# Second layer: the causal mask in spare rows of the exponent products, three products a round, and the second right side copied whole

## The chip, the cores and the metric

The kernel runs on one core of a Trainium2 chip, in one launch. The metric is the device time of that launch in microseconds (us). Engines are named as in the profile: PE (TensorE; PEld is its weight load), DVE (VectorE), ACT (ScalarE), POOL (GpSimd) and SP (SyncE), whose queue issues most of the transfers; POOL issues some too. Each engine works through its own instructions in order and waits on semaphores of the others.

## The reference

Two layers, each an attention over a context and a feed-forward part, on x of 8 x 256 tokens of width 512. Only the second layer's attention (an mLSTM with 16 heads of 32) is touched. For each batch row b and head:

```
ig = x_cat @ Wi + bi;   fg = x_cat @ Wf + bf
F  = cumsum(log_sigmoid(fg))
log_D[s,t] = F[s] - F[t] + ig[t]   for t <= s, else -inf
D  = exp(log_D - max_t log_D)
C  = (q @ k.T / sqrt(32)) * D
h  = (C / max(|sum_t C|, exp(-max))) @ v, then normed over each head
```

Row s attends to keys t <= s only. With 256 tokens cut in two halves of 128, the pair (second half of the keys, first half of the queries) is all masked and never computed; (first keys, first queries) and (second keys, second queries) hold the diagonal and need the mask; (first keys, second queries) needs none.

## The kernel before

The launch runs through these stages in the profile: the first layer's attention (to about 225 us), the first layer's feed-forward part with ternary weights, token tile by token tile, t = 0 to 15 (`layers_joined`, to about 357 us), the second layer's attention in 32 rounds (`layer1_rounds`, 357 to 503 us), and the second layer's shared and routed experts (to the end). In the second and third the order on every engine is written out by hand: `between(n, place)` looks up in the table `places` what else is issued at a given place of round n, and the profile's order is the program's.

A round n stands for one (b, k): batch row b = n // 4 and a group k = n % 4 of four heads. Its steps are spread over rounds: `decays` (round n) builds the exponents log_D - max with a product on PE and takes exp on ACT into a tile xe; `weights` (round n + 1) makes the products of queries and keys (pqk) and multiplies them by xe on DVE into ct; `heads` and `copied` (n + 2) make num and copy it; `back` (n + 3) turns it back. The per-row work that follows when a batch row is complete is `tail`: the head norms with a reciprocal root worked out on POOL (`rsqrt_aside`, L117 to L122), `scaled` and `attended` on POOL (L840, L847, L848: they add the result to x), layer-norm statistics on DVE (L129, L130, L923, L924), then the next b's root starts.

The exponent of a pair (t, s) is a sum of six numbers per head: three bf16 parts of the key's F and ig, three of the query's. `decays` gets it from one product: the stationary side `left` (g.left[b % 2], 128 rows x k x 256 keys) holds the key's parts in rows 0 to 11 (three parts for each of four heads) and ones in rows 12 to 14; the moving side `right` (g.right[b % 2], rows x k x head x 256 queries) holds in rows 0 to 11 a 0/1 pattern that picks the head, and in rows 12 to 14 the query's parts. KR = 15 rows are used, and rows 15 to 127 are zero on `left`. The mask is a second product on top, in the same PSUM tile pd: the identity times `lateb` (128 x 128, -1e30 where a query comes before a key), repeated over the heads. `decays` makes three such pairs of products and three exps of 128 x 512 a round: heads 0 and 1, first keys, all 256 queries, mask over the first 128 of each head (256 columns); the same for heads 2 and 3; and all four heads, second keys, second queries, mask over all 512 columns.

`lefts(b)` and `rights(b)` load the parts on SP's queue from `parts_d` in DRAM, where the gate chain has put them; for b = 0 they are issued in tile t = 15 of the feed-forward part, just ahead of the transposing transfer of the hidden tile of t = 14 (`hidden_rounded`, L1159, hq), for b + 1 in round 4b + 2. PE's product `output(14)` (py, L1165, 11 matmuls) stands in round 0 between the first two and the third exponent product, and waits for that transfer; `output(15)` stands at (2, 0).

There are two `left` tiles and two `right` tiles. The second `right` is made by `second_right` at place (2, 2), in the storage of the ternary weights w2 (tag wq2, free after `output(15)`): POOL sets 128 x 2048 words to zero, copies rows 0 to 11 from the first right by a transfer, and loads and scales `lns`. The storage of w3 (`held[1]`, free after the products of t = 15) serves as the third xe buffer `at["third"]`, taken by every n with n % 3 == 2; the others take the two buffers of the tag xe, which the feed-forward tiles' h used before.

`layer1_constants` makes lateb, the head pattern, and the left tiles on POOL at the start of the second stage; `layer1_right(k)` copies the head pattern into the four k of the first `right` on ACT, one each at t = 2 to 5.

Of the kernel before, what the change touches and what calls it, by code (L numbers as in the profile page):

```python
# [19 lines left out]
F32 = mybir.dt.float32  # L20
BF16 = mybir.dt.bfloat16
# [4 lines left out]
ALU = mybir.AluOpType  # L26
# [4 lines left out]
P = 128  # L31
D = 512
KD = D // P
B = 8
S = 256
T = B * S
NT = T // P
CH = 512
# [4 lines left out]
NF = FF // P  # L43
H1 = 16
HD1 = 32
# [606 lines left out]
HG = 4  # L652
KR = 3 * HG + 3


def layer1_constants(g, wp):
    nc = g.nc
    g.lateb = wp.tile([P, P], BF16, tag="lateb", name="lateb")
    nc.gpsimd.memset(g.lateb, 0.0)
    nc.gpsimd.affine_select(  # L660
        out=g.lateb, in_=g.lateb, compare_op=ALU.is_ge, fill=-1e30, base=0, pattern=[[1, P]], channel_multiplier=-1
    )
    g.head = wp.tile([P, HG], F32, tag="head", name="head")
    nc.gpsimd.memset(g.head, 0.0)
    for part in range(3):
        nc.gpsimd.affine_select(
            out=g.head, in_=g.head, compare_op=ALU.not_equal, fill=1.0, base=-HG * part, pattern=[[-1, HG]],
            channel_multiplier=1,
        )

    g.left = [wp.tile([P, KD, S], BF16, tag=f"left{n}", name=f"left{n}") for n in range(2)]
    g.right = [wp.tile([P, KD, HG, S], BF16, tag="right0", name="right0")]
    for left in g.left:
        nc.gpsimd.memset(left, 0.0)
        nc.gpsimd.memset(left[:KR], 1.0)
# [12 lines left out]
def layer1_rounds(g, tc, gates, work, ps, qp):  # L688
# [7 lines left out]
    def opened(held):  # L696
        row = 2 * H1 * (HD1 + 1)
        first = g.ctxT[0].rearrange("p k t -> p (k t)")
        for t in (held[0][:, :row], held[0][:, row : 2 * row], first[:, :row]):
            hid_of.append(t.rearrange("p (j h d) -> p j h d", j=2, h=H1))  # L700
        gates.em = held[0][:, 2 * row : 2 * row + 2 * P].rearrange("p (n q) -> p n q", n=2)
        at["third"] = held[1][:, : HG * (S + P)].rearrange("p (r s) -> p r s", r=HG)
        at["squared"] = held[1][:, HG * (S + P) :][:, : 2 * H1 * HD1]

    def second_right():
        more = qp.tile([P, NF * D // 2], F32, tag="wq2", name="held2")
        half = KD * HG * S // 2
# [4 lines left out]
        g.lns = more[:, half : half + D]  # L712
# [25 lines left out]
    def decays(b, k):  # L738


        keys, rows = g.left[b % 2][:, k], g.right[b % 2][:, k]
        if (b * KD + k) % 3 < 2:
            xe = work.tile([P, HG, S + P], F32, tag="xe", name="xe")
        else:
            xe = at["third"]

        def part(lhsT, rhs, late, out):
            pd = ps.tile([P, CH], F32, tag="dec", name="pd", bufs=2)
            n = rhs.shape[-1]
            pd = pd.rearrange("p (r s) -> p r s", s=n)  # L750
            nc.tensor.matmul(pd, lhsT=lhsT, rhs=rhs, start=True, stop=False)
            nc.tensor.matmul(
                pd[:, :, :P], lhsT=g.identb, rhs=lateb.unsqueeze(1).to_broadcast([P, CH // n, P]),
                start=False, stop=True,
            )
# [312 lines left out]
    class Rounds:  # L1068
        def second_right(self):
            second_right()  # L1070

        def lefts(self, b):
            lefts(b)

# [22 lines left out]
def layers_joined(g, tc, qp, gates):  # L1097
# [5 lines left out]
    with tc.tile_pool(name="f0a1", bufs=2, reuse_waits="tile") as work, tc.tile_pool(name="f0a1ps", bufs=1, space=PSUM, reuse_waits="tile") as ps:  # L1103
# [153 lines left out]
        with tc.manual_schedule(engines={E_.PE, E_.Activation, E_.DVE, E_.Pool, E_.SP}):  # L1257
# [15 lines left out]
            for t in range(NT):  # L1273
                front = t - 3
                roots = {6: 3, 7: 3, 10: 7}.get(t)
                if t:
                    hidden_scale(t - 1)
                products(t, 0)
                if 0 <= front < NT - 5:
                    added(front)  # L1280
                if t + 2 < NT:
                    largest(("x", t + 2), xn[t + 2])
                silu(t, 0)
                turn_next()
                gate_steps(t, 0)
                if t in (11, 12):
                    copy_next()
                if t:
                    shifted(("h", t - 1), h[t - 1])
                gated(t, 0)  # L1290
                if front >= NT - 5:
                    added(front)
                copy_next()
                if t == 11:
                    norm_next()
                if t + 2 < NT:
                    input_scale(t + 2)
                if front >= 0:
                    stats(front)
                rooted(roots, 3 if roots == 7 else 2)  # L1300
                gate_steps(t, 1)
                if t == 15:
                    rounds.lefts(0)
                    rounds.rights(0)
                products(t, 1)
                silu(t, 1)
                if t == 12:
                    gates.queries((0, 1))
# [49 lines left out]
            def turned(tag, engine=None):  # L1358
# [529 lines left out]
```

## Time and profile before

| what | value |
|---|---|
| median of 3 runs | 1054.01 us (1052.76 to 1054.7) |
| the profiled execution | 1053.98 us, span 1051.8 us, mean granted PE clock 0.984 |
| busy in the span: PE, DVE, ACT, POOL | 998.3, 532.3, 404.9, 394.3 us |
| the rounds, 357 to 503 us | 32 rounds; last exponent product 492.4 us |
| mask products (L752) in the rounds | 96, 29.5 us as single instructions |
| exponent products (L751) | 96, 35.0 us as single instructions |
| exps (L756) | 96, 53.8 us |
| second right: POOL memset, copy of 12 rows | 372.60 us for 1.81 us; issued 374.69 us |
| ACT's copies into the first right (L685) | 4, 1.03 us each, 246.4 to 268.9 us |

A matmul's own time in the profile holds its way through the array, so neighbours overlap; what a product adds to a row of products is read from the distance of starts in the timeline. A line such as `[1.66 <-DMA hq<-hq]` in the timeline is idle time of the engine just ahead of the instruction and what ended it. In the views by window, the columns are the window, its length, the busy time (and number of instructions) of PE, PEld, DVE, ACT and POOL, the clock granted to PE as a share of full speed, the busy share of the 16 DMA engines, and GB/s.

### The profile page before, as it was taken

To read this page: it belongs to the slowest core of one execution; us is meant where nothing else is said; L and a number is where in the kernel's file an instruction comes from. 1 tells how busy PE (TensorE), PEld (TensorE's weight loads), DVE (VectorE), ACT (ScalarE), POOL (GpSimd) and SP (SyncE) were. 2 spreads that over 40 slices of the span, in tenths; PEclk is the share of its full clock that TensorE was granted. 3 is DMA by queue.
4 is the path that set the end of the run, shared out by engine and by line. 5 is a ranking of instruction groups with operands and counts; after the bars stand their busy time and mean duration, and the time that the engine had idled before them with its cause. 6 is when DMAs were issued, how large, how long until landed. Compare 5 with 4: busy or idle time off the path is not lost.

```text
span 1051.8 us, 14757 instructions
## 1 busy us (share of the span) xinstructions
PE 998.3 (95%) x5210; PEld 607.5 (58%) x5210; DVE 532.3 (51%) x1417; ACT 404.9 (38%) x692; POOL 394.3 (37%) x452
## 2 busy tenths in 40 slices
PE   6999999979999899998998999999999999999994
PEld 5766666534444356665443445556666667778772
DVE  6546566679997768787828942112112121212120
ACT  4453443447687757876321001221222222221211
POOL 0023443450000114888203045554555556454522
PEclk9999999999999999999899999999999999999997
DMA  9663433323421411241112447777777778899972
GB/s 344 229 208 135 142 108 136 110 56 60 72 57 39 90 38 48 69 137 39 50 60 91 160 145 194 176 194 189 190 206 208 204 210 231 215 246 236 245 192 36
DMA packets 101011, 152.41 MB, mean 145 GB/s; under 512 B 39576, under 2 KB 42264, under 8 KB 100892
## 3 DMA queue, kind: packets, MB, share of 16 engines
q1 hardware_dynamic: 81984, 106.78, 32.4%
q0 software_dynamic: 18944, 44.60, 19.2%
q8 instruction: 43, 0.70, 0.3%
q14 instruction: 40, 0.33, 0.1%
HBM read 110.42 MB, written 32.96 MB: 136 GB/s over the span
## 4 chain that ended last, share of the span: by engine, by line
PE 74%; DVE 13%; POOL 4%; ACT 3%; issue 3%; DMA 1%; SPq 0%; POOLq 0%; DVEq 0%; ACTq 0%
PE po L1638 14%; PE pg L1621 13%; PE pu L1621 13%; PE pw L365 5%; PE pz L400 5%; PE pt L1678 3%; PE p L1118 2%; PE pgu L990 2%; DVE ct L779 2%; PE py L1165 2%; DVE h L1131 1%; PE pv L299 1%; DVE am L1135 1%; PE s L342 1%; PE pq L333 1%
## 5 line engine op out<-in xcount | busy, mean ns | idle before, releaser
L1626 DVE TENSOR_TENSOR act<-pu,sg 128x264 f32<-128x264 f32 (+22 forms) x68 | 31.9, 469 | 313.2 <-PE pu L1621 313.2
L1663 POOL DMA_INDIRECT xg<-h_d,tok_of x85 | 83.4, 981 | 197.9 <-DVE of L1673 64.8
L1682 POOL DMA_INDIRECT out_x<-eo,to x85 | 133.0, 1564 | 55.1 <-ACT eo L1720 34.4
L1638 PE MATMUL po<-w,act 128*128 128x512 f32 (+10 forms) x456 | 143.1, 489 | 0.0
L1621 PE MATMUL pg<-xT,w 128*128 128x216 f32 (+21 forms) x512 | 134.8, 406 | 0.8 <-issue 0.8
L1720 ACT ACTIVATE eo<-po,slotw 128x512 f32<-128x512 f32 (+10 forms) x114 | 65.6, 576 | 177.0 <-PE po L1638 170.6
L1621 PE MATMUL pu<-xT,w 128*128 128x216 f32 (+21 forms) x512 | 133.3, 403 | 0.0
L1621 PEld LDWEIGHTS pg<-xT,w 128*128 128x128 f32 x512 | 93.2, 190 | 33.2 <-issue 17.8
L1621 PEld LDWEIGHTS pu<-xT,w 128*128 128x128 f32 x512 | 96.8, 190 | 26.2 <-issue 5.6
L1625 ACT ACTIVATE sg<-pg 128x264 f32<-128x264 f32 (+22 forms) x68 | 28.5, 419 | 202.9 <-PE pg L1621 178.8
L1118 PE MATMUL p<-wq,xqT 128*128 128x512 bf16 (+1 forms) x384 | 81.2, 361 | 7.0 <-DVE qi L1139 6.2
L1638 PEld LDWEIGHTS po<-w,act 128*128 128x128 f32 (+10 forms) x456 | 54.2, 154 | 57.4 <-issue 47.9
L386 POOL TENSOR_TENSOR y<-y,gam 128x512 f32<-128x512 f32 x16 | 20.2, 1265 | 138.8 <-DVE y L83 138.8
L1118 PEld LDWEIGHTS <-xqT 128*128 128x128 bf16 x384 | 37.2, 98 | 49.4 <-issue 12.5
L1679 DVE TENSOR_TENSOR xT<-pt,nw 128x512 f32<-128x512 f32 (+12 forms) x85 | 51.1, 601 | 20.5 <-PE pt L1678 20.5
L400 PE MATMUL pz<-wo,wyT 128*128 128x512 f32 x128 | 59.5, 609 | 1.3 <-ACT wyT L395 1.3
L365 PE MATMUL pw<-wg,xnT 128*128 128x512 f32 x128 | 57.8, 594 | 0.0
L1678 PEld LDWEIGHTS pt<-ident,xg 128*128 128x128 f32 (+15 forms) x340 | 39.1, 140 | 23.9 <-PE po L1638 10.5
L129 DVE BATCH_NORM_STATS2 st<-x 128x6 f32<-128x512 f32 x64 | 43.9, 686 | 12.0 <-POOL x L848 6.3
L1678 PE MATMUL pt<-ident,xg 128*128 128x128 f32 (+15 forms) x340 | 47.2, 260 | 0.7 <-DVE xT L1679 0.6
L779 DVE SCALAR_TENSOR_TENSOR ct<-pqk,xe 128x768 f32<-128x768 f32 x44 | 40.0, 951 | 8.4 <-PE pqk L775 7.9
L1165 PE MATMUL py<-wq,hq 128*128 128x512 bf16 x176 | 42.3, 391 | 1.7 <-DMA hq<-hq 1.7
(336 smaller groups left out, 1680.7 us busy)
## 6 DMA issues: line engine op xcount, KB each, us to landing
w<-in_w SPq DMA_DIRECT2D x32, 1024.0 KB
w<-in_w SPq DMA_DIRECT2D x32, 512.0 KB
wst<-in_w1T SPq DMA_DIRECT2D x8, 704.0 KB
wst<-in_w3T SPq DMA_DIRECT2D x8, 704.0 KB
wst<-in_w2T SPq DMA_DIRECT2D x6, 768.0 KB
x<-in_x SPq DMA_DIRECT2D x16, 256.0 KB
ctxT<-in_ctxT_d SPq DMA_DIRECT2D x4, 1024.0 KB
raw<-in_ctx SPq DMA_DIRECT2D x16, 256.0 KB
```

The lines of the kernel that those rows point to most:

```text
L365: nc.tensor.matmul(pw, lhsT=xnT[c][:, k, o : o + P], rhs=wg[:, k, :], start=k == 0, stop=k == KD - 1)
L400: nc.tensor.matmul(pz[i], lhsT=wyT[i][:, k, :], rhs=wo[:, k, :], start=k == 0, stop=k == KD - 1)
L779: nc.vector.scalar_tensor_tensor(ct[:, r : r + 2, :], pqk[:, :, : S + P], 1.0 / math.sqrt(HD1), xe[:, r : r + 2, :], ALU.mult, ALU.mult,)
L1118: nc.tensor.matmul(both[:, m, : z - a], lhsT=xqT[:, k, :], rhs=w[:, k, a:z], start=k == 0, stop=k == KD - 1)
L1165: nc.tensor.matmul(py[t], lhsT=hqT[t][0][:, f, :], rhs=w2[:, f, :], start=f == 0, stop=f == NF - 1)
L1621: nc.tensor.matmul(pp[:, :n], lhsT=w[:, k, cols], rhs=xT[:, k, :n], start=k == 0, stop=k == KD - 1)
L1638: nc.tensor.matmul(po[h * at : h * at + n, :cols], lhsT=act[:, m, j * P : j * P + n], rhs=w[:, m, h * cols : (h + 1) * cols], start=m == 0 ...
L1663: nc.gpsimd.indirect_dma_start(out=xg[:n], out_offset=None, in_=h_d, in_offset=bass.IndirectOffsetOnAxis(ap=g.tok_of[:n, r, j : j + 1], ax ...
L1678: nc.tensor.transpose(pt[:, k, :n], xg[:n, k * P : (k + 1) * P], g.ident[:n, :n])
L1679: nc.vector.tensor_mul(xT, pt[:, :, :n], g.nw.unsqueeze(2).to_broadcast([P, KD, n]))
L1682: return nc.gpsimd.indirect_dma_start(out=g.out, out_offset=bass.IndirectOffsetOnAxis(ap=rows, axis=0), in_=eo, in_offset=None, compute_op ...
L1720: nc.scalar.activation(eo[:n, at : at + cols], po, AF.Copy, scale=w[r][:n, j : j + 1])
```

## The change

The mask of the diagonal pairs moves into rows 15 to 127 of the exponent product itself: `left` gets -1e30 in row p where the key's number in its half is p, and `right` gets 1 in row p for the queries s < p. That covers the keys 15 to 127; the first 15 rows are in use, so keys 0 to 14 still need a mask product, of KR - 1 = 14 query columns a head (lateb is cut to 128 x 14; 56 columns a product). The pair (first keys, second queries) must not have these rows: a third kind of stationary tile `open` (two of them, first half of the keys only) has the parts and ones in 15 rows and zeros below. A round now makes one product a pair of halves over all four heads: left x first queries with the small mask, open x second queries without a mask, left x second queries with the small mask. The exps stay three of 128 x 512.

`open` needs three more small transfers per batch row on SP's queue (12 rows of 256 bytes each, in `lefts`). The constants take more work on POOL (masked rows of both left tiles, and a whole head pattern with mask rows in k = 0 of the first right); ACT copies that k into the other three at t = 3 to 5, and nothing at t = 2. The second right is no longer set to zero: `second_right` moves to (0, 2), into the storage of w3, and copies rows 0 to 11 and rows 15 to 127 (113 rows of 8 KB) by two transfers of POOL's queue. The third xe buffer moves into the storage of w2, is set up at (2, 2), and is taken by n % 3 == 0 except n = 0.

```diff
+def opened_rows(g, n):
+    g.nc.gpsimd.memset(g.open[n], 0.0)
+    g.nc.gpsimd.memset(g.open[n][:KR], 1.0)
 def layer1_constants(g, wp):
-    g.lateb = wp.tile([P, P], BF16, tag="lateb", name="lateb")
+    g.lateb = wp.tile([P, KR - 1], BF16, tag="lateb", name="lateb")
...
+    g.open = [wp.tile([P, KD, P], BF16, tag="open0", name="open0")]
+    opened_rows(g, 0)
+    for left in g.left:
+        nc.gpsimd.memset(left, 0.0)
+        nc.gpsimd.affine_select(
+            out=left.rearrange("p k (j t) -> p (k j) t", t=P), in_=left.rearrange("p k (j t) -> p (k j) t", t=P),
+            compare_op=ALU.not_equal, fill=-1e30, base=0, pattern=[[0, 2 * KD], [-1, P]], channel_multiplier=1,
+        )
+        nc.gpsimd.memset(left[:KR], 1.0)
+    g.right = [wp.tile([P, KD, HG, S], BF16, tag="right0", name="right0")]
+    rows = g.right[0][:, 0]
+    nc.gpsimd.memset(rows, 0.0)
+    under = rows.rearrange("p r (j s) -> p (r j) s", s=P)
+    nc.gpsimd.affine_select(
+        out=under, in_=under, compare_op=ALU.is_ge, fill=1.0, base=0, pattern=[[0, 2 * HG], [1, P]], channel_multiplier=-1
+    )
+    nc.gpsimd.memset(rows[:KR], 0.0)
     for part in range(3):
         nc.gpsimd.affine_select(
-            out=g.head, in_=g.head, compare_op=ALU.not_equal, fill=1.0, base=-HG * part, pattern=[[-1, HG]],
+            out=rows, in_=rows, compare_op=ALU.not_equal, fill=1.0, base=-HG * part, pattern=[[-1, HG], [0, S]],
             channel_multiplier=1,
         )
 def layer1_right(g, k):
-    g.nc.scalar.copy(g.right[0][:, k], g.head.unsqueeze(2).to_broadcast([P, HG, S]))
+    g.nc.scalar.copy(g.right[0][:, k], g.right[0][:, 0])
 def opened(held):
-        at["third"] = held[1][:, : HG * (S + P)].rearrange("p (r s) -> p r s", r=HG)
-        at["squared"] = held[1][:, HG * (S + P) :][:, : 2 * H1 * HD1]
+        at["held"] = held[1]
+    def third():
+        more = qp.tile([P, NF * D // 2], F32, tag="wq2", name="held2")
+        at["third"] = more[:, : HG * (S + P)].rearrange("p (r s) -> p r s", r=HG)
+        at["squared"] = more[:, HG * (S + P) :][:, : 2 * H1 * HD1]
     def second_right():
-        more = qp.tile([P, NF * D // 2], F32, tag="wq2", name="held2")
         half = KD * HG * S // 2
-        nc.gpsimd.memset(more[:, :half], 0.0)
-        right = more[:, :half].bitcast(BF16).rearrange("p (k r s) -> p k r s", k=KD, r=HG)
-        nc.gpsimd.dma_start(out=right[: 3 * HG], in_=g.right[0][: 3 * HG])
+        right = at["held"][:, :half].bitcast(BF16).rearrange("p (k r s) -> p k r s", k=KD, r=HG)
+        for rows in (slice(0, 3 * HG), slice(KR, P)):
+            nc.gpsimd.dma_start(out=right[rows], in_=g.right[0][rows])
...
+        opened_rows(g, 1)
 def lefts(b):
...
+        for part in range(3):
+            nc.sync.dma_start(
+                out=g.open[b % 2][HG * part : HG * (part + 1)],
+                in_=parts_d[0, part, b * H1 : (b + 1) * H1, :P].rearrange("(k r) s -> r k s", r=HG),
+            )
 def decays(b, k):
-        if (b * KD + k) % 3 < 2:
+        n = b * KD + k
+        if n % 3 or n == 0:
             xe = work.tile([P, HG, S + P], F32, tag="xe", name="xe")
...
-        for r in range(0, HG, 2):
-            part(keys[:, :P], rows[:, r : r + 2, :], lateb, xe[:, r : r + 2, :S])
+        part(keys[:, :P], rows[:, :, :P], xe[:, :, :P])
+        part(g.open[b % 2][:, k], rows[:, :, P:], xe[:, :, P:S], False)
         yield xe
-        part(keys[:, P:], rows[:, :, P:], lateb, xe[:, :, S:])
+        part(keys[:, P:], rows[:, :, P:], xe[:, :, S:])
 layers_joined
-                if 2 <= t < 2 + KD:
+                if 2 < t < 2 + KD:
                     layer1_right(g, t - 2)
-                (0, 2): [partial(times, 1, first)],
+                (0, 2): [partial(times, 1, first), rounds.second_right],
-                (2, 2): [rounds.second_right],
+                (2, 2): [rounds.third],
```

More of the change, by code (lines that the diff above doesn't have):

```diff
@@ L653 @@
 KR = 3 * HG + 3
+def opened_rows(g, n):
+    g.nc.gpsimd.memset(g.open[n], 0.0)
+    g.nc.gpsimd.memset(g.open[n][:KR], 1.0)
 def layer1_constants(g, wp):
     nc = g.nc
-    g.lateb = wp.tile([P, P], BF16, tag="lateb", name="lateb")
+    g.lateb = wp.tile([P, KR - 1], BF16, tag="lateb", name="lateb")
     nc.gpsimd.memset(g.lateb, 0.0)
     nc.gpsimd.affine_select(
-        out=g.lateb, in_=g.lateb, compare_op=ALU.is_ge, fill=-1e30, base=0, pattern=[[1, P]], channel_multiplier=-1
+        out=g.lateb, in_=g.lateb, compare_op=ALU.is_ge, fill=-1e30, base=0, pattern=[[1, KR - 1]], channel_multiplier=-1
     )
-    g.head = wp.tile([P, HG], F32, tag="head", name="head")
-    nc.gpsimd.memset(g.head, 0.0)
+    g.left = [wp.tile([P, KD, S], BF16, tag=f"left{n}", name=f"left{n}") for n in range(2)]
+    g.open = [wp.tile([P, KD, P], BF16, tag="open0", name="open0")]
[15 more added lines that the diff above has]
+    nc.gpsimd.memset(rows[:KR], 0.0)
     for part in range(3):
         nc.gpsimd.affine_select(
-            out=g.head, in_=g.head, compare_op=ALU.not_equal, fill=1.0, base=-HG * part, pattern=[[-1, HG]],
+            out=rows, in_=rows, compare_op=ALU.not_equal, fill=1.0, base=-HG * part, pattern=[[-1, HG], [0, S]],
             channel_multiplier=1,
         )
[L671 to L675, printed above, removed]
     g.turn = wp.tile([P, HG, HD1 + 1], F32, tag="turn", name="turn")
@@ L701, in opened @@
         gates.em = held[0][:, 2 * row : 2 * row + 2 * P].rearrange("p (n q) -> p n q", n=2)
-        at["third"] = held[1][:, : HG * (S + P)].rearrange("p (r s) -> p r s", r=HG)
-        at["squared"] = held[1][:, HG * (S + P) :][:, : 2 * H1 * HD1]
+        at["held"] = held[1]
[3 more added lines that the diff above has]
+        at["squared"] = more[:, HG * (S + P) :][:, : 2 * H1 * HD1]
     def second_right():
-        more = qp.tile([P, NF * D // 2], F32, tag="wq2", name="held2")
         half = KD * HG * S // 2
-        nc.gpsimd.memset(more[:, :half], 0.0)
-        right = more[:, :half].bitcast(BF16).rearrange("p (k r s) -> p k r s", k=KD, r=HG)
-        nc.gpsimd.dma_start(out=right[: 3 * HG], in_=g.right[0][: 3 * HG])
+        right = at["held"][:, :half].bitcast(BF16).rearrange("p (k r s) -> p k r s", k=KD, r=HG)
+        for rows in (slice(0, 3 * HG), slice(KR, P)):
+            nc.gpsimd.dma_start(out=right[rows], in_=g.right[0][rows])
         g.right.append(right)
-        g.lns = more[:, half : half + D]
+        g.lns = at["held"][:, half : half + D]
+        g.open.append(at["held"][:, half + D :][:, : KD * P // 2].bitcast(BF16).rearrange("p (k t) -> p k t", k=KD))
+        opened_rows(g, 1)
         nc.gpsimd.dma_start(out=g.lns, in_=g.ln_scale.partition_broadcast(P))
@@ L745, in decays, with part @@
             xe = at["third"]
[L747 to L755, printed above, removed]
+        def part(lhsT, rhs, out, masked=True):
+            pd = ps.tile([P, CH], F32, tag="dec", name="pd", bufs=2).rearrange("p (r s) -> p r s", s=P)
+            nc.tensor.matmul(pd, lhsT=lhsT, rhs=rhs, start=True, stop=not masked)
+            if masked:
+                few = lateb.shape[-1]
+                nc.tensor.matmul(
+                    pd[:, :, :few], lhsT=g.identb, rhs=lateb.unsqueeze(1).to_broadcast([P, HG, few]),
+                    start=False, stop=True,
+                )
             nc.scalar.activation(out, pd, AF.Exp)
-        for r in range(0, HG, 2):
-            part(keys[:, :P], rows[:, r : r + 2, :], lateb, xe[:, r : r + 2, :S])
+        part(keys[:, :P], rows[:, :, :P], xe[:, :, :P])
+        part(g.open[b % 2][:, k], rows[:, :, P:], xe[:, :, P:S], False)
         yield xe
-        part(keys[:, P:], rows[:, :, P:], lateb, xe[:, :, S:])
+        part(keys[:, P:], rows[:, :, P:], xe[:, :, S:])
         yield xe
@@ L1070, in second_right, with third @@
             second_right()
+        def third(self):
+            third()
         def lefts(self, b):
```

## The prediction

> **What bounds the kernel now.** I read the page's head first: PE is busy 998.3 of 1051.8 us, which says little of a stage. Then the busy time by window over the rounds, the only stage whose instructions change much:
>
> ```profile
> 400.00:410.00 10.00, 9.92 (x119) 6.40 (x117) 9.54 (x18) 5.84 (x14) 1.68 (x4) 1.00 0.03 8
> 480.00:500.00 20.00, 16.88 (x206) 11.47 (x206) 14.90 (x25) 13.05 (x28) 17.88 (x29) 1.00 0.11 41
> ```
>
> At 400 us DVE (third busy figure) is as full as PE; at 480 POOL (fifth) is the fullest. A full PE does not decide here, so next the chain of waits in that stretch (start, length, what):
>
> ```profile
> 481.05 0.70 DVE st L129
> 481.87 1.19 DVE var L833
> 483.06 1.73 DVE ct L779 x2
> 484.79 0.61 DVE st L129
> ...
> 487.05 0.30 POOL var L117
> ...
> 496.06 1.20 POOL x L848
> 497.29 0.70 DVE st L129
> ```
>
> From one `st` to the next, 16.2 us for four rounds, there is only DVE and POOL: statistics, the root, `scaled`, `attended`, statistics again. The `st` that closes a lap starts at 434.27, 449.73, 465.17, 481.05 and 497.29 in the timeline: laps of 15.4 to 16.2 us. So PE's time is hidden from 434 on. POOL's part of that lap begins with L117 at 424.67, after DVE work that runs without a gap from here:
>
> ```profile
> 398.07 1.82 DVE L779 SCALAR_TENSOR_TENSOR ct<-pqk,held 128x768 f32<-128x768 f32 x2 [1.65 <-PE pqk L775]
> ```
>
> This is the last place where DVE waits over 1 us for PE before that unbroken run. What PE saves before 398.07 moves the rest forward; what it saves later does not.
>
> **What PE saves.** One undisturbed round in PE's timeline:
>
> ```profile
> 429.16 0.39 PE L751 MATMUL pd<-held,left 128*128 128x512 bf16 x1
> 429.39 0.27 PE L752 MATMUL pd<-lateb,identb 128*128 128x256 bf16 x1
> 429.50 0.38 PE L751 MATMUL pd<-held,left 128*128 128x512 bf16 x1
> 429.71 0.27 PE L752 MATMUL pd<-lateb,identb 128*128 128x256 bf16 x1
> 429.82 0.63 PE L807 MATMUL back<-turn,numT 128*128 128x132 f32 x4
> 430.35 0.38 PE L751 MATMUL pd<-held,left 128*128 128x512 bf16 x1
> 430.56 0.38 PE L752 MATMUL pd<-lateb,identb 128*128 128x512 bf16 x1
> 430.87 0.73 PE L771 MATMUL pqk<-qT,ctxT 32*128 32x256 f32 x8
> ```
>
> By distance of starts the masks take 0.11, 0.11 and 0.31 us, the products 0.22 each. The three products stay. Two masks of 56 columns replace three; no such row exists. From above one costs what the 256-column one does, 0.11; from below 56/256 of it, 0.02. I take 0.10, since each stands between two weight loads of 98 ns (L752 PEld, mean) that so short a product cannot cover. About 0.10 of the third mask's 0.31 is the way into the next load and stays. Saved a round: 0.53 - (0.10 + 0.20) = 0.23, from 0.20 to 0.39; I use 0.25.
>
> Where it counts: round 0's third product and round 1 (0.35 together: ACT's exp waited 1.15 us for that mask), round 2 up to pqk at 373.33 (0.25), then nothing, because DVE's root of the last tiles (376 to 379.6) releases qT and PE's num waits 0.89 for it at 380.47; then rounds 4, 5 and 6 (0.75). Sum 1.35, with the per-round bounds and the ACT-bound places 0.8 to 2.1. I take **-1.3**. The other 25 rounds save 6.3 us of PE that the DVE and POOL laps hide; without that cover they would be worth all of it.
>
> **What the moved copy costs.** `second_right` goes to (0, 2). Its first transfer waits for PE's last reader of w3, which ends as py(13) starts, 354.71. POOL is free since 351.8, so it issues at 354.9 and, at 0.61 us an issue (L710), the 113 rows at 355.5. In the packet records of the trace data follows the issue by 1.2 us (vc_d) to 2.0 us (the 12 rows of before): from 356.7 to 357.5. There stands:
>
> ```profile
> 356.28 1.41 SPq L1159 DMA_TRANSPOSE hq<-hq  x1
> 358.20:359.80 1.60, 0.00 (x0) 0.00 (x0) 1.53 (x5) 0.35 (x1) 0.00 (x0) 1.00 0.89 175
> 359.86 4.23 PE L1165 MATMUL py<-wq,hq 128*128 128x512 bf16 x11 [1.66 <-DMA hq<-hq]
> 360.40:363.80 3.40, 3.40 (x10) 1.22 (x8) 3.13 (x13) 2.98 (x4) 0.00 (x0) 0.50 0.18 67
> q0 software_dynamic: 112, 0.36, 10.7%
> ```
>
> The transposing transfer of tile 14 keeps the DMA engines 0.89 busy, PE has nothing to do but wait for it, and then runs py(14) at half clock: 11 matmuls in 4.2 us that take 2.5 elsewhere. Whatever delays hq delays everything. The last line (POOL's queue, 374 to 384 us) prices the copy: 0.36 MB took 10.7% of 16 engines for 10 us, 17 engine-us; 113 rows of 8 KB are 0.93 MB, 44 engine-us, or 2.8 us of all 16. If it queues behind hq it costs 0; if hq gets nothing until it is through, 2.8. I take half of that and a little, 1.6, as both are under way together. Then PE's clock: with py starting at 361.5, a clock back at 363.8 ends it at 365.1 (+1.2); a second half-speed stretch ends it at 366.2 (+2.3), with up to 0.6 more in what follows. In 500.3 to 503.7 PE was busy 2.46 of 3.40 us and the next 3.4 us were still at 0.50, and here it would be busy 2.3 of 3.4. So I take **+2.0**, with 0 and +4.2 as ends.
>
> [...]
>
> **The rest.** POOL's constants grow: about 8 memsets and selects of 1024 columns more (memset 0.95 us each, L674; a select of 128 columns 0.30, so 0.3 to 2.4 for 1024, I take 1.1). They ended at 235.05, now near 243.5, at worst 252; ACT first reads them at 254.5, so the cover is 10 us. But POOL then runs beside DVE, and one and the same DVE operation (L823) lasts 181 ns at best and 1469 beside POOL. Two or three such stalls of 1 us could fall on tiles 1 and 2, where PE has products ahead: 0 to 1.5, I take **+0.3**. ACT's copy dropped at t = 2 (1.03 us) frees ACT where it then waits 1.82 for PE: 0. The three `open` transfers add 0.9 us on SP (0.30 each, as `left`) between 354.74 and hq's issue; `right` already waited until 355.21 for parts_d, and hq for ACT until 356.26, so they fit with 0.3 to spare (0 to +0.3); raw behind them is needed at 374.8. In later batch rows nothing follows them for two rounds. The new wait of POOL holds back only its memsets, lns (first used at 416) and the `open` loads of b = 1 on SP at 365. xe of round 2 now waits for ct of round 0, which ends at 370.65 where the exp starts at 370.56: 0.1, hidden.
>
> Sum on the profiled 1053.98: -1.3 + 2.0 + 0.3 = +1.0, so 1055.0; the median, 1054.01, is the same.
>
> **The rivals.**
> - *The copy starves hq (34%).* Every small packet of hq waits behind an 8 KB one for the full 2.8 us: py starts at 362.7, at half clock throughout, 4.7 us, ends at 367.4 instead of 363.9: +3.5, and with the port stalls and -1.3 about +2.6 to +4: 1057.2. For it: hq's packets are many and small. It decides from about 2.3 us of delay to hq. Slower.
> - *The copy misses hq (18%).* Its data start after 359.2, or transfers share without loss: -1.3 + 0.3, to 1051.9 at best: 1052.9. For it: the 12 rows of before started 2.0 us after issue and lns 2.9.
> - *PE is the bound in all rounds (12%).* The page's 74% PE in the chain would say so: 32 x 0.25 = 8, less 1 to 2 for hq: 1047. Against it: the laps, and `st` waiting for POOL 6.3 us in five places.
> - *My forecast (36%)*: a partial delay, 1053.4 to 1056.2.
>
> **How the numbers follow.** About 0.2% (2.1 us) is what can be told from no change. The forecast gives 28 within it, 8 slower; the starved case 33 slower, 1 within; the missed one 12 within, 6 faster; the PE bound 12 faster. So faster 0.18, same 0.41, slower 0.41. The range leaves out the PE bound and the worst of the starved case: 1051.9 to 1058.0.
>
> **What would show it.** The start of py(14), 359.86 before: 361 to 362 for the forecast, 362.5 or later for the starved case, unchanged for the missed one. The granted clock from 360 to 367. The place of DVE's ct of 398.07: 1 us later on balance, and the same distances of `st` from there on. PE's idle time in later rounds should grow by 0.25 a round. I am wrong if laps shorten below 15.4 us, or if DVE operations around 240 us lengthen by more than 1.5 us together.

## The result, and the profile after

| | before | after |
|---|---|---|
| median of 4 runs, us | 1054.36 | 1068.22 |
| profiled execution, its span | 1051.8 | 1066.6 |
| granted TensorE clock | 0.984 | 0.977 |
| start of py(13), of py(14) | 354.71, 359.86 | 357.92, 373.96 |
| the ct with which DVE's unbroken run begins | 398.07 | 411.40 |
| first pgu | 505.40 | 518.67 |

The ratio is 1.0136, with an interval of 1.0122 to 1.0150: slower by 14 us, and outside the range. By the table 3.2 us are lost before py(13), 10.9 more between py(13) and py(14), 0.8 comes back up to ct, nothing changes until pgu, and 1.5 go behind it. The two losses have places of their own. The later one first, in the timeline of the kernel after (start, length, engine, instruction, and in brackets the idle time before it and what ended it):

```profile
357.92 2.54 PE L1196 MATMUL py<-wq,hq 128*128 128x512 bf16 x11
...
358.38 1.16 POOL L730 DMA_DIRECT2D held<-right  x2 [3.38 <-PE p L1149]
...
359.49 4.22 SPq L1190 DMA_TRANSPOSE hq<-hq  x1
...
373.96 4.61 PE L1196 MATMUL py<-wq,hq 128*128 128x512 bf16 x11 [10.37 <-DMA hq<-hq]
```

SP issues the transposing transfer 1.57 us after py(13) starts, exactly as before (356.28 against 354.71). What follows is not as before: the issue sits 4.22 us in the queue where it took 1.41, and PE waits 10.37 us for the data where it waited 1.66. The busy time by window (PE, PEld, DVE, ACT, POOL, granted clock, DMA share, GB/s) shows what the chip does meanwhile, and the two lower rows answer to those of 400 and 480 us:

```profile
361.00:373.60 12.60, 0.62 (x3) 0.23 (x3) 6.30 (x22) 3.93 (x4) 0.19 (x1) 0.64 1.12 144
374.00:378.40 4.40, 4.40 (x12) 1.54 (x12) 0.00 (x0) 0.00 (x0) 1.29 (x1) 0.53 0.78 186
413.33:423.33 10.00, 9.72 (x117) 6.55 (x115) 9.54 (x18) 5.59 (x14) 1.69 (x4) 1.00 0.03 9
493.27:513.27 20.00, 16.01 (x199) 10.87 (x191) 14.89 (x25) 12.52 (x27) 17.89 (x29) 1.00 0.11 41
```

For 12.6 us PE does 0.62 us of work while the DMA engines count as more than full (a share of 1.12) and move only 144 GB/s; then py(14) runs at half clock. In the lower rows DVE and POOL are as full as before, and PE has more idle time: 16.01 busy of 20 us, where it had 16.88. So the products did get cheaper, and it bought nothing there. DVE's own rows say the same:

```profile
411.40 1.82 DVE L807 SCALAR_TENSOR_TENSOR ct<-pqk,xe 128x768 f32<-128x768 f32 x2 [1.46 <-PE pqk L803]
...
463.02 0.69 DVE L129 BATCH_NORM_STATS2 st<-x 128x6 f32<-128x512 f32 x1 [1.42 <-POOL x L876]
...
478.47 0.69 DVE L129 BATCH_NORM_STATS2 st<-x 128x6 f32<-128x512 f32 x1 [1.69 <-POOL x L876]
...
494.34 0.69 DVE L129 BATCH_NORM_STATS2 st<-x 128x6 f32<-128x512 f32 x1 [1.98 <-POOL x L876]
...
510.56 0.69 DVE L129 BATCH_NORM_STATS2 st<-x 128x6 f32<-128x512 f32 x1 [1.97 <-POOL x L876]
```

Before, the same `st` stood at 449.73, 465.17, 481.05 and 497.29. Each is 13.3 us later, and the laps are the same to 0.02 us. One round of PE after:

```profile
436.87 0.38 PE L777 MATMUL pd<-held,left 128*128 128x512 bf16 x1
437.08 0.19 PE L780 MATMUL pd<-lateb,identb 128*128 128x56 bf16 x1
437.20 0.73 PE L799 MATMUL pqk<-qT,ctxT 32*128 32x256 f32 x8
...
438.88 0.39 PE L777 MATMUL pd<-held,left 128*128 128x512 bf16 x1
439.10 0.19 PE L780 MATMUL pd<-lateb,identb 128*128 128x56 bf16 x1
439.13 0.38 PE L777 MATMUL pd<-held 128*128 128x512 bf16 x1
```

From start to start the two masks take 0.12 and 0.03 us. Before, three took 0.11, 0.11 and 0.31: a round saves 0.38 us.

The earlier loss lies between 225 and 250 us, where POOL makes its constants. In the timeline of the kernel after:

```profile
237.13 1.45 DVE L1180 TENSOR_TENSOR s<-qi,iw 128x1 f32<-128x1 f32 x1
...
237.48 1.09 POOL L684 TENSOR_SCALAR_AFFINE_SELECT right<-right 128x1024 bf16<-128x1024 bf16 x1
...
239.63 3.99 POOL L689 TENSOR_SCALAR_AFFINE_SELECT right<-right 128x1024 bf16<-128x1024 bf16 x3
...
240.01 0.71 DVE L1210 TENSOR_SCALAR s<-iw,qi 128x2 f32<-128x2 f32 x1
...
242.22 0.59 PE L1149 MATMUL p<-wq,xqT 128*128 128x512 bf16 x2 [0.87 <-DVE h L1162]
```

and the same two DVE operations in the timeline of the kernel before:

```profile
235.66 0.14 DVE L1149 TENSOR_TENSOR s<-qi,iw 128x1 f32<-128x1 f32 x1
...
237.23 0.21 DVE L1179 TENSOR_SCALAR s<-iw,qi 128x2 f32<-128x2 f32 x1
```

An operation on one column lasts 1.45 us instead of 0.14, and ends at 238.58, when POOL's select ends (238.57).

### The profile page after: what moved, and what is told of

Read it like the earlier page. It is cut to its first block, busy times and chain, and to the rows that moved or that the text cites. A ratio compares the mean times of both kernels' runs of the same rounds, so it can differ in the third digit from the quotient of the medians.

```text
span 1066.6 us, 14732 instructions
## 1 busy us (share of the span) xinstructions
PE 994.1 (93%) x5178; PEld 605.5 (57%) x5178; DVE 536.7 (50%) x1417; ACT 402.2 (38%) x691; POOL 403.1 (38%) x460
## 4 chain that ended last, share of the span: by engine, by line
PE 68%; DVE 16%; POOL 5%; ACT 4%; issue 3%; DMA 2%; SPq 0%; DVEq 0%; POOLq 0%; ACTq 0%
PE po L1669 13%; PE pg L1652 12%; PE pu L1652 12%; PE pw L365 5%; PE pz L400 5%; PE pt L1709 3%; PE pgu L1018 2%; PE p L1149 2%; DVE ct L807 2%; DVE h L1162 2%; DVE am L1166 2%; PE py L1196 2%; PE pv L299 1%; DMA hq<-hq 1%; DVE st L129 1%
## 5 line engine op out<-in xcount | busy, mean ns | idle before, releaser
L1709 PEld LDWEIGHTS pt<-ident,xg 128*128 128x128 f32 (+15 forms) x340 | 39.2, 140 | 23.9 <-PE po L1669 10.5
L784 ACT ACTIVATE xe<-pd 128x512 f32<-128x512 f32 x66 | 37.4, 603 | 17.1 <-PE pd L780 16.9
```

Source lines behind the costliest of these rows:

```text
L1709: nc.tensor.transpose(pt[:, k, :n], xg[:n, k * P : (k + 1) * P], g.ident[:n, :n])
```

## The experiments

Eleven kernels, one of them run a second time, each beside runs of the kernel before on the same chip. "Gap" is the time from the start of py(13) to that of py(14) in the profile: 5.15 before, 16.04 after.

| run | what differs | median | before | ratio, interval | gap |
|---|---|---|---|---|---|
| e1_copy_late | after, copy behind py(15) | 1057.47 | 1052.62 | 1.0042, 1.0029-1.0056 | 5.22 |
| e2_copy_112 | after, 113 rows as 1 + 112 | 1060.36 | 1052.62 | 1.0070, 1.0052-1.0089 | 10.21 |
| e3_no_113 | after, no copy of 113 rows | 1057.95 | 1052.62 | 1.0052, 1.0036-1.0067 | 7.30 |
| e4_before_constants | before, POOL's added work | 1056.24 | 1052.62 | 1.0033, 1.0021-1.0044 | 5.16 |
| e5_copy_127 | after, 112 + 1 from row 15 | 1064.46 | 1054.67 | 1.0092, 1.0076-1.0107 | 12.75 |
| e6_copy_by_k | after, four transfers | 1068.37 | 1054.67 | 1.0142, 1.0126-1.0157 | 14.11 |
| e7_small_constants | e1, POOL's constants short | 1055.62 | 1054.67 | 1.0017, 1.0006-1.0028 | 5.22 |
| e9_half_copy | after, half the bytes | 1059.23 | 1053.94 | 1.0053, 1.0037-1.0070 | 7.88 |
| e7_again | e7 once more | 1056.68 | 1053.94 | 1.0023, 1.0014-1.0032 | 5.17 |
| e8_wide_masks | e7, masks of 512 columns | 1055.38 | 1053.94 | 1.0017, 1.0008-1.0026 | 5.32 |
| e10_behind_hq | e7, copy behind the last hq | 1054.47 | 1054.13 | 1.0007, 0.9998-1.0015 | 5.17 |
| e11_113_first | after, the two transfers swapped | 1063.93 | 1054.13 | 1.0102, 1.0085-1.0118 | 13.08 |

**The copy taken out of hq's way.** The move alone is undone; the storages of the second right side and of the third xe change places:

```diff
 def second_right():
+    at["held"] = qp.tile([P, NF * D // 2], F32, tag="wq2", name="held2")
...
-    (0, 2): [partial(times, 1, first), rounds.second_right],
+    (0, 2): [partial(times, 1, first)],
...
-    (2, 2): [rounds.third],
+    (2, 2): [rounds.second_right],
```

> Second right side back in the third weight's storage at (2, 2), so that its copy can only start once py(15) has run; third in held[1] from the start; everything else as changed. Theory 'the copy in flight starves hq': py(14) starts within 0.5 us of py(13)'s start + 5.2 (it was +5.15 before the change, +16.04 after), and the kernel takes 1068.2 - 10.9 = 1057.3 us (1056.5 to 1058.5, a little more if round 4 now waits for its right side). Rival 'something else of the change holds hq (the open loads on SP, the small masks)': py(14) stays at +14 or more and the time at 1066 to 1069.

The timeline of PE in this run, py(14) and round 4's first products:

```profile
363.37 4.12 PE L1197 MATMUL py<-wq,hq 128*128 128x512 bf16 x11 [1.08 <-DMA hq<-hq]
...
385.76 0.38 PE L778 MATMUL pd<-held,left 128*128 128x512 bf16 x1 [1.49 <-DMA held<-parts_d]
```

py(13) started at 358.15, so the gap is back to 5.22: the 10.8 us go with what was moved to (0, 2), that is the copy, the load of `ln_scale` issued behind it (`lns` in the prediction, 64 packets of 4 KB) and POOL's two fills. The late copy has a smaller price of its own: round 4 waits 1.49 us for its right side.

**What in the copy costs it.** Two kernels split the 113 rows, one drops them (the zeroing on POOL of the kernel before stands in, and the mask of the odd batch rows is left out), all else as in the changed kernel:

```diff
-for rows in (slice(0, 3 * HG), slice(KR, P)):
+for rows in (slice(0, 3 * HG), slice(KR, KR + 1), slice(KR + 1, P)):
```

> The copy of 113 rows issued as 1 row and 112 rows, same bytes, same place, one issue (0.6 us) more. Theory 'the row count decides' (113 rows go to few engines, 112 spread evenly): the 8 KB packets are through in about 3 us and not 9.7, py(14) starts at py(13) + 8 at most, and the time is 1059 to 1062 us. Rival 'large packets in front of small ones, however they are spread': py(14) at +14 to +17, time 1066 to 1070.

```diff
-for rows in (slice(0, 3 * HG), slice(KR, P)):
-    nc.gpsimd.dma_start(out=right[rows], in_=g.right[0][rows])
+nc.gpsimd.memset(at["held"][:, :half], 0.0)
+nc.gpsimd.dma_start(out=right[: 3 * HG], in_=g.right[0][: 3 * HG])
```

> The copy of the 113 rows is left out (the mask of the odd batch rows is missing from the output); in its place stands the zeroing on POOL that the kernel before had, and the 12 rows are copied as there. If the bytes of the large copy are what starves hq: py(14) at py(13) + 5 to +6.5 (POOL's zeroing runs beside DVE) and 1057 to 1058.5 us. If the 12 rows, ln_scale or the issue on POOL's queue are enough to hold hq, it stays at +10 or more and 1063 or more.

```diff
-for rows in (slice(0, 3 * HG), slice(KR, P)):
+for rows in (slice(0, 3 * HG), slice(KR, P - 1), slice(P - 1, P)):
```

> The 113 rows again as 112 and 1, but the 112 now start at row 15, where the 113 did, and the single row is the last one. The run with rows 15 and 16 to 127 took 1060.4 us, py(14) 10.2 us after py(13). Theory 'it is the number 113': as there, 1060 to 1061 us and 10 to 10.5. Rival 'it is where the rows begin' (row 15 against row 16): as the changed kernel, 1067 to 1069 us and about 16.

Neither pure theory holds. With 112 rows from row 16 the gap is 10.21, with 112 from row 15 it is 12.75, with the 113 together 16.04: the same bytes at the same place differ by up to 5.8 us by their layout, and neither the number 113 nor the first row alone decides. Without the 113 rows 2.1 us of the gap remain. The packet records place them: hq's last packet ends 4.61 us after the start of py(13), as in the kernel before (4.62), so no data come late; but the semaphore that releases PE takes its last step 2.64 us after that packet, where it took 0.49 before. POOL's zeroing had ended by then (358.55, hq's first packet 359.29); the 12 rows and the load of `ln_scale` were in flight.

The packet records show it us by us. For each us of the span, the 256-byte packets of hq that ended, and the copy's of 8 KB:

```
before            357: 395      358: 803      359: 210
112 and 1 rows    359: 2 / 17   360: 30 / 35  361: 38 / 38  362: 239 / 28  363: 234 / 6  364: 684 / 0  365: 180 / 0
after             360: 0 / 4    361: 63 / 30  362: 6 / 23   363: 6 / 24    364: 35 / 19  365: 199 / 13
                  366: 42 / 1   367: 139 / 6  368: 250 / 5  369: 427 / 0   370: 151 / 0  371: 55 / 0   372: 34 / 0
```

Undisturbed, hq's 1408 packets end within 1.9 us. Beside the copy hq at first gets about one packet of 256 bytes for each of 8 KB (68 against 73 in the two us from 360, second row), so most of it, 899 of its packets there and 878 in the third row, ends only when the copy is through. In the third row the copy also has a tail: from 366 a few packets, single ones of up to 4.1 us, are still under way, and hq gets 42 to 250 a us until 368.5.

The wait does not end with the copy. Its last packet ends at 368.52 in the third row, and the 878 packets of hq still to come, 1.1 us at the 800 a us of the first row, take until 373.04. The packets of `ln_scale` run from 368.82 to 373.05 beside them; in the second row they start at 365.10, when hq is nearly through. Of the 5.8 us between these two layouts 3.4 are the copy's own, 2.9 come behind it, and the semaphore takes 0.5 back. No run took the load of `ln_scale` away by itself, so its part is not shown.

Then the bytes themselves, in shorter packets and by half (with half of them, the mask of half the heads of the odd batch rows is left out, and the 12 rows go behind):

```diff
-for rows in (slice(0, 3 * HG), slice(KR, P)):
-    nc.gpsimd.dma_start(out=right[rows], in_=g.right[0][rows])
+nc.gpsimd.dma_start(out=right[: 3 * HG], in_=g.right[0][: 3 * HG])
+for k in range(KD):
+    nc.gpsimd.dma_start(out=right[KR:, k], in_=g.right[0][KR:, k])
```

> The same 113 rows as four transfers, one for each k, so with packets of 2 KB in place of 8 KB and three issues (1.7 us) more. Theory 'the length of the packets in front of hq's 256 bytes decides': hq interleaves better, py(14) at py(13) + 8 or less, 1058 to 1060 us, in spite of 113 rows. Theory 'the number 113 decides': each of the four is spread as badly, py(14) at +14 or more, 1066 to 1069 us.

```diff
-for rows in (slice(0, 3 * HG), slice(KR, P)):
-    nc.gpsimd.dma_start(out=right[rows], in_=g.right[0][rows])
+nc.gpsimd.dma_start(out=right[KR:, : KD // 2], in_=g.right[0][KR:, : KD // 2])
+nc.gpsimd.memset(at["held"][:, half // 2 : half], 0.0)
+nc.gpsimd.dma_start(out=right[: 3 * HG], in_=g.right[0][: 3 * HG])
```

> The copy of the 113 rows carries two of the four k alone, half its bytes, at its place of the changed kernel (the other half is zeroed on POOL, so the mask of half of the odd batch rows' heads is missing). Theory 'hq moves only when the copy is through': with half the bytes the delay of py(14) halves, from 10.9 to 4.5 to 6.5 us over the undisturbed 5.15 after py(13), and the kernel takes 1061 to 1063.5 us where before is 1054. Rival 'a fixed cost of having such a transfer in flight': the delay stays at 9 or more, 1066 or more.

Four transfers go out as packets of 4 KB for the most part, and the gap is 14.11: packets of half the length help little. Half the bytes cost 2.7 us of gap, less than either theory expected, and the records show no tail there. The gap is no clean price of the bytes, as it is 2.1 us without any of them: the last packet of hq comes 1.5 us later than before with half the bytes, 4.2 later with the evenly spread whole, and 10.5 later with the 113 rows; the rest is the late semaphore. Last, the order:

```diff
-for rows in (slice(0, 3 * HG), slice(KR, P)):
+for rows in (slice(KR, P), slice(0, 3 * HG)):
```

> The changed kernel with its two transfers in the other order, the 113 rows first and the 12 rows behind them. Half the bytes of the 113 rows, with the 12 rows behind, delayed py(14) by 2.7 us, a quarter of the whole copy's 10.9. Theory 'the 12 rows ahead, which fill 12 engines, cause the late packets': the delay falls to 5 to 6 us, py(14) at py(13) + 10 to 11.5, time 1060 to 1063. Rival 'the whole copy of 113 rows has them anyway': py(14) at +14 or more, 1066 to 1069.

13.08, between the two: the order matters by 3 us, and the 12 rows ahead are not the tail's only cause. In the kernel before, the 12 rows are 12 packets, all under way at 377.3; which engines they fill the records do not say. What makes the tail stays open.

**The constants.** The kernel before, with the added POOL work on tiles whose values do not change:

```diff
...
 for left in g.left:
     nc.gpsimd.memset(left, 0.0)
+    nc.gpsimd.affine_select(
+        out=left.rearrange("p k (j t) -> p (k j) t", t=P), in_=left.rearrange("p k (j t) -> p (k j) t", t=P),
+        compare_op=ALU.not_equal, fill=0.0, base=0, pattern=[[0, 2 * KD], [-1, P]], channel_multiplier=1,
+    )
     nc.gpsimd.memset(left[:KR], 1.0)
+rows = g.right[0][:, 0]
+nc.gpsimd.memset(rows, 0.0)
...
+nc.gpsimd.memset(rows[:KR], 0.0)
+for part in range(3):
+    nc.gpsimd.affine_select(
+        out=rows, in_=rows, compare_op=ALU.not_equal, fill=0.0, base=-HG * part, pattern=[[-1, HG], [0, S]],
+        channel_multiplier=1,
+    )
```

> The kernel before, with the added POOL constants alone: the same selects and fills of 512 and 1024 columns at the same place of the program, on tiles whose values stay as they were. Theory 'POOL beside DVE in tiles 0 to 2 costs 3.2 us': py(13) starts at 357.9 (354.7 before) and the time is 1057.2 us (1056.5 to 1058). Rival 'the constants are hidden, as the prediction had it (0.3), and the shift ahead of py(13) comes from elsewhere': py(13) at 355.0, time 1054.0 to 1054.6.

3.5 us by the ratio, 2.1 in the profile (py(13) at 356.82). Its timeline:

```profile
235.63 1.08 POOL L678 TENSOR_SCALAR_AFFINE_SELECT left<-left 128x1024 bf16<-128x1024 bf16 x1
...
235.92 0.81 DVE L1168 TENSOR_TENSOR s<-qi,iw 128x1 f32<-128x1 f32 x1
...
238.16 1.41 DVE L1198 TENSOR_SCALAR s<-iw,qi 128x2 f32<-128x2 f32 x1
...
238.46 1.09 POOL L686 TENSOR_SCALAR_AFFINE_SELECT right<-right 128x1024 bf16<-128x1024 bf16 x1
...
241.08 2.10 PE L1137 MATMUL p<-wq,xqT 128*128 128x512 bf16 x8 [1.58 <-DVE h L1150]
```

Both `s` end with POOL's select (236.73 and 236.71; 239.57 and 239.55), and PE waits for the DVE work behind them. In the nine profiles with these constants py(13) is 1.4 to 2.1 us late where PE's clock is whole from 226 to 250 us, and 1.8 to 3.4 where a window there is at half speed (after: 231.4 to 234.8, and the 24 matmuls of one p last 6.59 us and not 4.91).

The counterpart makes POOL's instructions short: it selects 128 columns at most, and ACT spreads them. It stands on the late copy:

```diff
...
+g.diag, g.under = g.open[0][:, 0], g.left[1][:, 0, :P]
+for one, op, fill, step, few in ((g.diag, ALU.not_equal, -1e30, -1, 1.0), (g.under, ALU.is_ge, 1.0, 1, 0.0)):
+    nc.gpsimd.memset(one, 0.0)
+    nc.gpsimd.affine_select(
+        out=one, in_=one, compare_op=op, fill=fill, base=0, pattern=[[step, P]], channel_multiplier=-step
+    )
+    nc.gpsimd.memset(one[:KR], few)
...
+    g.nc.scalar.copy(
+        g.left[n].rearrange("p k (j t) -> p (k j) t", t=P), g.diag.unsqueeze(1).to_broadcast([P, 2 * KD, P])
+    )
...
+        for r in range(HG):
+            g.nc.scalar.activation(
+                g.right[0][:, 0, r].rearrange("p (j s) -> p j s", s=P),
+                g.under.unsqueeze(1).to_broadcast([P, 2, P]), AF.Identity, bias=g.head[:, r : r + 1],
+            )
```

> The late copy of the first run, and the long POOL constants made small: POOL fills and selects 128 columns at most, and ACT spreads them over left, open and right by broadcast (two copies of 1024 columns, one of 512, four of 256, at t = 2, 6, 8 and 10). Values as in the changed kernel. Theory 'DVE operations are held by the long POOL instructions, and nothing else of the constants costs': 1057.5 - 3.5 = 1054.0 us on the scale of the first measurement, 1052 to 1053 where before is 1052.6; py(13) at 354.7 or earlier. What is left between it and before is the products and masks alone: by the first run's profile about -0.4. Rival 'the added constants cost through ACT or through what waits for POOL': at 1056 or more, py(13) at 357.

py(13) is at 354.49, 0.2 earlier than before. `s` and its select in the timeline of this run:

```profile
228.22 0.29 POOL L675 TENSOR_SCALAR_AFFINE_SELECT open<-open 128x128 bf16<-128x128 bf16 x1
...
235.44 0.14 DVE L1194 TENSOR_TENSOR s<-qi,iw 128x1 f32<-128x1 f32 x1
...
237.01 0.21 DVE L1224 TENSOR_SCALAR s<-iw,qi 128x2 f32<-128x2 f32 x1
```

So the constants cost only through the long instructions. But the median is 0.17% above before and not at or below it, and the runs spread from 1053.8 to 1059.2 us.

**What the products and masks alone are worth.** With both costs out of the way:

> The kernel with the late copy and the small constants once more, to be compared with the next one on one chip. Its 11 runs went from 1053.8 to 1059.2 us, those at a granted clock of 0.983 from 1053.8 to 1055.2. Theory 'the clock gate takes back what PE saves': again 1054 to 1059, median 0.5 to 1.5 above before. Rival 'chance of that chip': within 0.3 of before, or below it.

```diff
-g.lateb = wp.tile([P, KR - 1], BF16, tag="lateb", name="lateb")
+g.lateb = wp.tile([P, P], BF16, tag="lateb", name="lateb")
...
```

> The same kernel, but its two masks a round add 128 columns of each head again (512 in all) and not 14 (56 in all): 0.6 to 0.7 us of PE a round given back, about all of what the change saves there and a little more; values unchanged. Theory 'what PE saves is worth 0.4 to 0.7 us up to round 6 and hidden behind DVE and POOL from there': ct of round 6 is 0.4 to 1.5 us later than in the run before it, the laps stay at 15.4 to 16.2, and the time is 0.5 to 1.5 us more. Theory 'the clock gate takes it back': fewer half-clock windows, and the same time or less. Rival 'PE bounds the rounds': 32 x 0.6 = 19 us more.

The first stays 0.23% above before, more than either theory gave. From e7_again, py(14) and the ct of 398.07:

```profile
359.91 4.23 PE L1210 MATMUL py<-wq,hq 128*128 128x512 bf16 x11 [1.12 <-DMA hq<-hq]
...
382.24 0.38 PE L791 MATMUL pd<-held,left 128*128 128x512 bf16 x1 [1.43 <-DMA held<-parts_d]
...
397.59 1.82 DVE L821 SCALAR_TENSOR_TENSOR ct<-pqk,xe 128x768 f32<-128x768 f32 x2 [1.46 <-PE pqk L817]
```

and from e8_wide_masks:

```profile
359.84 2.55 PE L1210 MATMUL py<-wq,hq 128*128 128x512 bf16 x11 [1.03 <-DMA hq<-hq]
...
397.93 1.82 DVE L821 SCALAR_TENSOR_TENSOR ct<-pqk,xe 128x768 f32<-128x768 f32 x2 [1.65 <-PE pqk L817]
```

The wide masks bring ct 0.34 us later, 0.56 counted from py(13), where 0.4 to 1.5 was expected. Their median is 1.3 us less where 0.5 to 1.5 more was expected, with intervals that overlap: they cost nothing that shows. PE bounding the rounds is out. In the profile of the wide masks the granted clock is 0.987 and four windows before the last stretch are at half speed; in e7_again it is 0.983 and six, among them the one in which py(14) takes 4.23 us in place of 2.55. That fits the theory recorded for e7_again, that a clock gate takes back what PE saves; with overlapping intervals it is not shown.

The last kernel puts the copy where neither hq nor round 4 meets it: POOL reads a column of the hq of t = 15 before it issues the copy, which goes out as 12, 1 and 112 rows.

```diff
...
+nc.gpsimd.tensor_copy(at["held"][:, half : half + 1], behind)
+nc.gpsimd.tensor_copy(right[:, 0, 0, :1], at["held"][:, half : half + 1])
...
+(0, 2): [partial(times, 1, first), lambda: rounds.second_right(hqT[late][0][:, 0, :1])],
```

> Small constants, full saving of the masks, and the second right side back in held[1], but POOL now reads one column of tile 15's hq before it issues the copy (rows 0 to 11, 15, and 16 to 127), so that the copy starts when the last hq has landed, at about 367, with no hq beside it and 5 us earlier than in the runs with the late copy. There round 4's first product waited 1.25 to 1.43 us for its right side. Theory 'the late copy is what is left of the change's cost': that wait goes, py(14) stays at py(13) + 5.2, ct of round 6 at 396.5 to 397.4 (397.59 and 397.93 there, 398.07 before), and the median is 0 to 1 us below before. Theory 'the clock gate takes back what is saved': 0.5 to 2.5 us above before, as the runs there, with a granted clock of 0.979 to 0.983 against 0.985.

```profile
366.84 0.19 POOL L742 CAST held<-hq 128x1 f32<-128x1 bf16 x1 [15.27 <-DMA hq<-hq]
...
381.27 0.39 PE L792 MATMUL pd<-held,left 128*128 128x512 bf16 x1
...
384.43 0.63 PE L792 MATMUL pd<-held,left 128*128 128x512 bf16 x1
```

Its timeline shows POOL waiting for hq, round 4 no longer waiting for its right side, and a product at 384.43 that lasts 0.63 us in place of 0.38, in a half-clock window from 382.3 which the kernel before does not have; so its ct is at 399.04, not at the 396.5 to 397.4 expected. The granted clock of its runs is 0.979 to 0.984, that of before on the same chip 0.984 to 0.986. The median is 1.0007 of before, 0.9998 to 1.0015: freed of both costs, the change neither loses nor gains what can be measured. None of the kernels beats the one before.

## Why the prediction failed, step by step

- **What bounds the rounds: right.** From ct on DVE and POOL go round in laps of 15.4 to 16.2 us that no run changed (the same to 0.02 us in the profile after); the 25 later rounds' saving is hidden.
- **PE's saving: the size of a round and the number of rounds, wrong in opposite directions.** 0.38 us a round, at the upper bound of 0.39, where 0.25 was taken. By ct the changed kernel has gained 0.8 us, where -1.3 stood. In e7_again, whose py(14) lasts 4.23 us as before, the 0.6 forecast up to `num` of 380.47 is there in full (py(14) at 359.91, `num` at 379.95); in the changed kernel 0.2 of it, as its py(14) lasts 0.4 longer. From round 4's first product (381.26 before, 395.16 after) to ct 0.6 of 0.75 come. So without the longer py(14) nearly the forecast sum is there, but as the saving of three rounds of 0.38 and not of over five of 0.25: that the sums are close is luck. e1_copy_late keeps 0.4 (3.44 late at py(13), 3.04 at ct), with round 4 waiting for its right side.
- **The copy's +2.0: the term that failed.** It measures 10.9, undone by e1_copy_late. The place, the waiter and the issue times were right: the data start 1.6 us after py(13) (2.0 to 2.8 expected) and the `open` loads fit ahead of hq's issue. Three sub-steps were wrong. The price: 44 engine-us over 16 engines, 2.8 us, came from a row with 12 packets of 8 KB and 64 of 4 KB; alone, in e1_copy_late, the same transfers lasted 6.2 us (377.1 to 383.4) with a median packet of 0.56 us. The halving, "as both are under way together": one small packet for each large one (68 to 73) leaves hq with little, so nearly the whole length counts, and this was the assumption of the rival with 34%, which fits the counts, though at 1057.2 it too fell far short. And what 113 rows cost over 1 and 112, 5.8 us: the copy's tail and the slow end of hq beside `ln_scale`, which no row of before showed and no rival had; the prediction counted `lns` only as held back. py(14) at half clock, 4.61 us, was foreseen in kind.
- **How the rows went out.** That the 113 rows spread over all 16 engines was the author's estimate, and the packet records of the kernel after come near to it: 9 to 15 of the copy's packets, mostly 13 or 14, were under way at a time from 360.5 to 365. One behind another they would have taken 113 x 0.31 = 35 us (an estimate from the shortest packet), and the whole copy took 9. That 113 rows go to few engines, a theory recorded for e2_copy_112, does not fit this. Why hq gets about one packet for each of the copy's no run shows; the runs give only the price.
- **POOL's constants at +0.3: the other term that failed.** 3.2 us at py(13) in the profile after; 3.5 by the ratio of e4_before_constants, 2.1 in its profile. "ACT first reads them at 254.5, so the cover is 10 us" covered the constants and not DVE. The prediction itself had seen a DVE operation grow from 181 to 1469 ns beside POOL and then granted two or three stalls under PE's cover; but in tiles 0 to 2 PE waits for DVE (0.20, 0.87). In the rows above `s` ends with POOL's select to 0.02 us (238.58 and 238.57 after, 236.73 and 236.71, 239.57 and 239.55 in e4_before_constants). Which of the two started first does not decide it: `s` at 237.13 starts 0.35 us ahead of the select that it ends with, while a fill of POOL's (236.57 to 237.51) still runs. What holds DVE there no run shows; the "port stalls" of the first rival are these stalls, and no run shows a port.
- **Not foreseen at all:** 1.5 us behind 518 us, 0.8 of it by 569 us and 0.7 in the last stretch, after PE's shift has settled at 14.06. No run was made on them.
- Read off the two profiles, the sum is -0.8 + 10.9 + 3.2 + 1.5 = 14.8. As stretches of the same two spans these add up by construction; e1_copy_late and e4_before_constants confirm the 10.9 and, roughly, the 3.2.

## What to carry to other kernels

When a transfer is moved, look first at which transfer that PE waits for is on the DMA engines at that moment, charge about the moved one's whole length to it, not its share of the bandwidth, and look at what is issued behind it: here hq's last packet came 10.5 us later beside a copy of 9 us and 4.2 later beside one of 5.6. Long POOL instructions beside a DVE that PE waits for cost here up to 1.3 us for a short DVE operation that they met (1.45 us in place of 0.14); 128 columns and a broadcast by ACT left it at 0.14 and py(13) at 354.49. And a saving on an engine that waits elsewhere is worth only the few places where that engine is waited for: of 0.38 us in each of 32 rounds, 0.8 us had arrived at ct, and no more by the first pgu.

## What the runs showed of the hardware

- One and the same copy of 1.02 MB (125 packets of 8 KB) from SBUF to SBUF lasts 6.2 us without hq beside it (e1_copy_late; 4.8 when its 113 rows are issued as 1 and 112 from row 16, e10_behind_hq), and beside hq 9 us as 113 rows (after) and 5.6 as 1 and 112 (e2_copy_112); single 8 KB packets take 0.31 to 4.1 us (after). Why the layout matters that much is open.
- A transposing transfer of 0.36 MB, 1.9 us alone (before), got 2 to 38 of its 1408 packets a us up to 362 while that copy ran as 1 and 112 rows (e2_copy_112), and 0 to 63 up to 365 as 113 (after), where it gets some 800 undisturbed.
- The semaphore of that transfer takes its last step 0.5 us after its last packet when POOL's queue moves nothing beside it (before), and 2.6 us after it with the 12 rows and `ln_scale` in flight (e3_no_113).
- A mask product of 56 columns between two products costs 0.03 us from start to start (after, 439.10), less than the 0.10 that the prediction took for it.
- Of kernels with the same work the one with more PE work had fewer half-clock windows (e8_wide_masks against e7_again: four against six before the last stretch, a granted clock of 0.987 against 0.983), and its time was no longer (1055.38 against 1056.68, with intervals that overlap).
